# Image scores copied out by VectorE instead of ScalarE, and the second pair's norm products and rounding issued ahead of a slot's last filler work, in a two-layer image-prompted cross-attention

## The chip, the cores and the metric

The kernel runs on one core of one Trainium2 chip. The time is the device time of one execution in microseconds (us). Three runs of the kernel before gave a median of 1542.27 us, from 1538.93 to 1542.37 us.

## The reference

Two cross-attention layers follow each other on 16 images of 256 query rows and 320 channels, with 20 heads of 16 channels. The context of an image has 252 text tokens and 4 image tokens of 512 channels. The second layer, which is the one that the change touches, computes (cut to what matters):

```python
q = heads(hidden_states @ W_q)                       # also k_t, v_t, k_ip, v_ip from the context
probs_t = softmax(einsum('bhsd,bhtd->bhst', q, k_t) * attn_scale)
text_out = einsum('bhst,bhtd->bhsd', probs_t, v_t)
attn_scores = einsum('bhsd,bhnd->bhsn', q, k_ip) * attn_scale
qsem = l2norm(einsum('bhst,bte->bhse', probs_t, text_ehs))
sem = einsum('bhse,bne->bhsn', qsem, l2norm(ip_ehs))
probs_ip = softmax(attn_scores + 0.5 * sem) * spatial_mask
out = (text_out + einsum('bhsn,bhnd->bhsd', probs_ip, v_ip)) @ W_out + b_out + residual
```

The norm of `qsem` is not computed from `qsem`: with the Gram matrix G of the text tokens, its square is p G p for each row p of the (not yet normalized) probabilities.

## The kernel before, in words

The work is cut into slots. A slot k is one image and four heads: slots 0 to 79 belong to layer 0, slots 80 to 159 to layer 1, five to an image, so that 16 images follow each other with five slots each. The main loop (L1139) goes through the parts of `slot1(k)` in order. A part that is a function issues instructions; a part that is a number n calls `fill(k + n)`, which issues all filler work that is due by then: the next image's keys and tokens (`prod`, L212), query and output projections (`project`, L520), and the rest. TensorE's instructions stay in the order in which they are issued. The order on VectorE, ScalarE and GpSimd is made by a scheduler that honours data dependencies and the manual ones that `queued` adds: `anchor(x)` remembers an instruction as the last anchored one of its engine, `queued(x)` puts x behind that one.

In slot k of layer 1 the following happens.

- `both1(k, t)` for the two halves t of 128 rows: the turned scores of slot k (L788, tiles `T`, two PSUM banks) and the row scores of slot k + 2 (L793, tile `S`, two banks, of which there is one only). VectorE takes the row maxima of the text scores from `S` (L794). ScalarE takes the exponentials of the turned scores (L799). `image_scores` copies the 4 image scores of each of the four heads, 16 numbers in each partition, out of `S` into `sr` (L811, on ScalarE). The matmuls of half 1 into `S` can begin when both readers of half 0 are done.
- `attend1(k - 2)`, between the two halves: probabilities times values (L862) and, as the last term of the same sum, the squared norms (L864). Its second operand `wt` is summed by GpSimd for pair u = 0 and by VectorE for pair u = 1 (L854).
- `rounded1(k, u)`: ScalarE rounds the exponentials to a narrow type (L839, tile `ctb`, two of them), GpSimd takes the remainder (L840, tile `wt`).
- `norm1(k - 1, u, n)`: the product with one block column of the Gram matrix G (L849, four matmuls for n = 0, three for n = 1); VectorE multiplies it with `wt` (L852) and the two columns are added (L854).
- `maxima(k + 2)`: the maxima are transposed (L827), cast by ScalarE (L829) and sent by two DMAs from ScalarE's queue into the rows of `qs` (L831).

Of the filler work, these lines play a part below: `keys1`, where ScalarE casts and VectorE subtracts (L147, L148, tile `kst`); `tokens1`, which makes the values and the Gram matrix of the next image (L478 to L499, tiles `v1t` and `gm`; L499 is VectorE's last read of its last PSUM tile); and the split of the context (L147 and L148 on GpSimd, tile `cta`).

The PSUM tiles are declared with one to three buffers each, but the eight banks are handed out anew as tiles are asked for (`auto_bufs`), so that a tile's bank can be the one that any other kind of tile has left.

Of the kernel before, what the change touches and what calls it, by code (L numbers as in the profile page):

```python
# [10 lines left out]
AF = mybir.ActivationFunctionType  # L11
# [17 lines left out]
SCALE = 0.25  # L29
# [8 lines left out]
NS = B * NG  # L38
# [10 lines left out]
def xattn2(  # L49
# [27 lines left out]
    nc = tc.nc  # L77
# [11 lines left out]
    def bank(tag="X"):  # L89
        return ps.tile([128, 512], F32, tag=tag, name=tag, bufs=BANKS[tag])  # L90

    def scores():

        return ps.tile([128, 1024], F32, tag="S", name="S", bufs=1).rearrange("p (h t) -> p h t", h=4)
# [4 lines left out]
    def buf(tag, shape, dtype=F32, bufs=1, name=None):  # L99
        if tag in ("wB", "wD", "vr", "raw"):  # L100
            return sb.tile(shape, dtype, tag=tag, name=name or tag, bufs=bufs)
        size = 1
        for d in shape[1:]:
            size *= d
        if tag not in slots:
            slots[tag] = [0, dtype] + [const_tile([128, max(size, words.get(tag, 0))], f"{tag}_{i}", dtype) for i in range(bufs)]
        n, kind, *ring = slots[tag]
        assert kind == dtype and len(ring) == bufs, tag
        slots[tag][0] += 1
        t = ring[n % bufs][: shape[0], :size]  # L110
        names = "abcd"[: len(shape) - 1]
        if len(names) > 1:
            t = t.rearrange(f"p ({' '.join(names)}) -> p {' '.join(names)}", **dict(zip(names, shape[1:])))
        return t
# [17 lines left out]
    def queued(inst, *behind):  # L132

        for other in behind or [anchors.get(inst.ins.engine)]:
            if other is not None:
                tc.add_manual_dep(
                    inst.ins, other.ins.name, mybir.DependencyInfo(mybir.DependencyClass.NoSync, mybir.DependencyReason.DATA), reason="order"
                )
        return inst

    def anchor(inst):
        anchors[inst.ins.engine] = inst
        return inst
# [460 lines left out]
    QK, P, W, R = {}, {}, {}, {}  # L604
# [76 lines left out]
    def attend0(k):  # L681
        b, g = divmod(k, NG)
        v, pv = get("v0", b), bank("P")
        for vt in range(3):
            values0(k, pv, v, vt)
        settle0(b, g, pv)
# [87 lines left out]
    def both1(k, t):  # L774

        a = k + 2 < 2 * NS and QK[k + 2] 
        c = NS <= k < 2 * NS and QK[k]
        if a:
            if t == 0:
                maxes[k + 2] = buf("mn", [128, 4, 4], FR, bufs=2)[:, :2]  # L780
            sp = scores()
        if c:
            st = [bank("T").rearrange("p (h t) -> p h t", h=2) for u in range(2)]
            lo = (0, DUP)[t]
            for j in range(2):
                for u in range(2):
                    rows = slice(64 * u, 64 * u + KS1)
                    mm(st[u][:, j], c[1][rows, j, lo : lo + 128], c[0][rows, j], start=True, stop=True)  # L788
        if a:
            for j in range(2):  # L790
                for u in range(2):
                    rows = slice(64 * u, 64 * u + XROW)
                    mm(sp[:, 2 * u + j], a[0][rows, j, t * 128 : (t + 1) * 128], a[1][rows, j], start=True, stop=True)  # L793
            anchor(nc.vector.tensor_reduce(maxes[k + 2][:, t], sp[:, :, :T1], axis=AX.X, op=ALU.max))  # L794
        if c:
            for u in range(2):
                if t == 0:
                    P[k, u] = buf("P", [128, 2, 2, S], bufs=SIZES["NP"]) if (k - NS) % 3 else last_stack([128, 2, 2, S], F32, u)
                anchor(queued(nc.scalar.activation(P[k, u][:, t], st[u], AF.Exp, scale=SCALE)))  # L799
        if a:  # L800
            image_scores(k + 2 - NS, t, sp)

    sims = {}

    def image_scores(n, t, sp):
        b, g = divmod(n, NG)
        if (g, t) == (0, 0):
            sims[b] = buf("sr", [128, 2, 4, NG, NIP], bufs=2)
        sr = sims[b]
        src = sp.rearrange("p (u j) t -> p u j t", u=2)[:, :, :, T1:]  # L810
        anchor(nc.scalar.copy(sr[:, t, :, g].rearrange("p (j u) n -> p u j n", u=2), src))  # L811
        if (g, t) == (NG - 1, 1):
            later(0.3, lambda: image_scores_out(b))

    def image_scores_out(b):
        sid = dram.tile([S, 4, NG * NIP], F32, tag="sid", name="sid", bufs=2)
        dma(sid.rearrange("(t p) s c -> p t (s c)", p=128), sims[b].rearrange("p t s g n -> p t (s g n)"))
        si = results["si", b] = buf("si", [128, 8, NG * NIP], bufs=2)
        parts = sid.rearrange("(f r) s c -> r s f c", r=32)
        for s in range(4):  # L820
            later(1.3, lambda s=s: dma(si[32 * s : 32 * s + 32], parts[:, s]))
# [13 lines left out]
    def rounded1(k, u):  # L835
        R[k, u] = buf("ctb", [128, 2, 2, S], FR, bufs=SIZES["CTB"], name="ph")
        W[k, u] = buf("wB", [128, 2, 2, S], bufs=SIZES["WB"], name="wt")
        for t in range(2):
            nc.scalar.activation(R[k, u][:, t], P[k, u][:, t], AF.Copy, scale=0.5)  # L839
            anchor(nc.gpsimd.tensor_sub(W[k, u][:, t], P[k, u][:, t], f(R[k, u][:, t])))  # L840
# [3 lines left out]
    def norm1(k, u, n):  # L844

        gm = get("t1", k // NG - B)[1]
        yp = bank().rearrange("p (h t) -> p h t", h=2)
        for i, (gb, kt) in enumerate(blocks[n]):
            mm(yp, gm[:, gb], R[k, u][:, kt], start=i == 0, stop=i == len(blocks[n]) - 1)  # L849
        w = W[k, u]  # L850
        product = yp if n and u else w[:, n]
        nc.vector.tensor_mul(product, yp, w[:, n])  # L852
        if n:
            (nc.vector if u else nc.gpsimd).tensor_add(w[:, 0], w[:, 0], product)  # L854

    def attend1(k):
        b, g = divmod(k - NS, NG)
        v, pv = get("t1", b)[0], bank("P")
        for n in range(2):
            for s in range(4):  # L860
                h = V1W * (4 * g + s)
                mm(pv[32 * s : 32 * s + 32, :S], v[:, n, h : h + 32], P[k, s % 2][:, n, s // 2], start=n == 0, stop=False)  # L862
        for s in range(4):
            mm(pv[32 * s : 32 * s + 32, :S], zone, W[k, s % 2][:, 0, s // 2], start=False, stop=True)  # L864
        settle1(b, g, pv)

    def slot1(k):
        last = k - 1 if NS < k <= 2 * NS else None
        mine = k < 2 * NS
        if k == NS:  # L870
            yield lambda: maxima(k + 1)
        yield lambda: both1(k, 0)
        if k == NS:
            yield lambda: attend0(k - 1)
        if k > NS + 1:
            yield lambda: attend1(k - 2)
        yield lambda: both1(k, 1)
        if last:
            yield lambda: norm1(last, 0, 0)
        yield 0.33  # L880
        if last:
            yield lambda: norm1(last, 0, 1)
        if mine:
            yield lambda: rounded1(k, 0)
        yield lambda: stacks(k + LEAD)
        if last:
            yield lambda: norm1(last, 1, 0)
        yield 0.67
        if last:
            yield lambda: norm1(last, 1, 1)  # L890
        if mine:
            yield lambda: rounded1(k, 1)
        yield lambda: maxima(k + 2)
        yield 1.0

# [124 lines left out]
    def later(slots, make):  # L1020
        delayed.append((clock[0] + slots, make))
# [26 lines left out]
    for c in range(B // 2):  # L1048
        n, k = 10 * c, [("k0", c)] if c else []
# [11 lines left out]
    for b in range(B):  # L1061
        n = NS + 5 * b
# [17 lines left out]
    def stacks(k, parts="KQ"):  # L1080
        if 0 <= k < NS:
            stacks0(k, parts)
        elif k < 2 * NS and "K" in parts:
            stacks1(k)

    def ahead(k, t):
        if k < NS:
            score0(k, t)
        else:
            both1(k - 2, t)  # L1090

    def maxima(k):
        if k < 2 * NS:
            (maxima0 if k < NS else maxima1)(k)
# [43 lines left out]
    with tc.manual_schedule(engines=PINNED):  # L1138
        for k in range(2 * NS + 2):  # L1139
            clock[0] = k  # L1140
            for part in (slot0 if k < NS else slot1)(k):
                if callable(part):
                    part()
                else:
                    fill(k + part)
        fill(999)
# [81 lines left out]
```

## Time and profile before

| | |
|---|---|
| median of 3 runs | 1542.27 us |
| the profiled execution | 1542.67 us |
| its span, first to last instruction | 1540.9 us |
| VectorE busy | 1167.0 us (76%) |
| ScalarE busy | 966.5 us (63%) |
| GpSimd busy | 1144.5 us (74%) |

The profile names engines PE (TensorE's matmuls), PEld (its weight loads), DVE (VectorE), ACT (ScalarE), POOL (GpSimd) and SP (SyncE, whose rows here are DMA issues). A row of a timeline has the start in us from the span's start, the duration in us, engine, line, operation, the tiles written and read, the shape, how often, and in square brackets the idle time ahead of it with what ended it. Layer 1 runs from about 700 us to the end.

### The profile page before, as it was taken

Reading aid. Unit: us, or ns where it says so; the run is one execution under the profiler, and the core shown is the slowest. Engines: PE = TensorE matmul, PEld = TensorE weight load, DVE = VectorE, ACT = ScalarE, POOL = GpSimd, SP = SyncE. Lnnn points to the kernel's source line nnn. Section 1 sums busy time; section 2 is a strip of 40 time slices with the busy share of each in tenths; the row PEclk is TensorE's granted clock in tenths of the full one; section 3 lists DMA queues with packets and bytes.
Section 4 is the critical chain, followed back from the end, with each engine's and each line's share of the span. In section 5 each row is a group of like instructions: output and inputs, shape, how many; then the busy total and the mean of one; then the engine's idle time right before and its main releaser. Section 6 shows DMA issues by size and latency. Waiting matters only on the chain.

```text
span 1540.9 us, 35237 instructions
## 1 busy us (share of the span) xinstructions
PE 1461.3 (95%) x12522; PEld 1194.7 (78%) x12522; DVE 1167.0 (76%) x2424; ACT 966.5 (63%) x2233; POOL 1144.5 (74%) x1161
## 2 busy tenths in 40 slices
PE   7789999999999998899999999999999999999997
PEld 6778888888888887677777777777777777777765
DVE  5457676767776778877888788878877887888796
ACT  5557676767676766656656555655665566556562
POOL 3259797979797867886777777777777787777685
PEclk9899999999999999999999999999999999999999
DMA  7656565656565665464424443434344434433311
GB/s 218 164 170 173 161 173 165 176 164 178 156 192 144 169 195 134 122 195 145 142 80 142 117 135 107 132 114 146 104 136 120 136 111 129 127 110 107 110 34 57
DMA packets 226971, 215.38 MB, mean 140 GB/s; under 512 B 49714, under 2 KB 210708, under 8 KB 226796
## 3 DMA queue, kind: packets, MB, share of 16 engines
q1 hardware_dynamic: 225056, 211.83, 47.9%
q8 instruction: 100, 1.64, 0.5%
q10 hardware_dynamic: 1740, 1.30, 0.3%
q14 instruction: 75, 0.61, 0.1%
HBM read 122.17 MB, written 89.49 MB: 137 GB/s over the span
## 4 chain that ended last, share of the span: by engine, by line
PE 61%; DVE 12%; ACT 7%; POOL 7%; DMA 7%; issue 3%; ACTq 2%; SPq 1%; POOLq 0%; DVEq 0%
PE X L212 19%; PE X L849 10%; PE X L520 8%; PE P L711 7%; PE S L650 5%; DVE mn L794 4%; PE T L673 4%; POOL wt L840 3%; PE S L793 2%; ACT ctb L839 2%; ACTq L831 2%; POOL wt L854 1%; DMA sid<-sr 1%; POOL cta L148 1%; PE X L569 1%
## 5 line engine op out<-in xcount | busy, mean ns | idle before, releaser
L679 POOL TENSOR_TENSOR P<-P,rs 128x512 f32<-128x512 f32 x320 | 412.1, 1310 | 158.8 <-ACT P L676 158.7
L840 POOL TENSOR_TENSOR wt<-P,ctb 128x512 f32<-128x512 f32 x212 | 270.8, 1296 | 94.5 <-ACT ctb L839 93.5
L849 PE MATMUL X<-ctb,gm 128*128 128x512 f32 x1120 | 308.8, 405 | 0.4 <-DVE ho L750 0.4
L676 ACT ACTIVATE P<-T 128x512 f32<-128x512 f32 x320 | 174.8, 593 | 103.8 <-PE T L673 94.6
L849 PEld LDWEIGHTS X<-ctb,gm 128*128 128x128 f32 x1120 | 195.8, 188 | 41.3 <-DVE ho L750 0.6
L794 DVE TENSOR_REDUCE mn<-S 128x4 fp32r<-128x1008 f32 x160 | 191.0, 1194 | 18.1 <-PE S L793 17.7
L852 DVE TENSOR_TENSOR wt<-X,wt 128x512 f32<-128x512 f32 x240 | 164.4, 686 | 38.7 <-PE X L849 36.7
L839 ACT ACTIVATE ctb<-P 128x512 fp32r<-128x512 f32 x212 | 124.8, 626 | 45.5 <-PE X L849 43.2
L652 DVE TENSOR_REDUCE mn<-S 128x4 fp32r<-128x716 f32 x160 | 142.4, 890 | 0.0
L711 PE MATMUL P<-P,vr 128*32 128x256 f32 x1920 | 123.8, 388 | 4.8 <-DVE mx L575 2.6
L799 ACT ACTIVATE P<-T 128x512 f32<-128x512 f32 x212 | 114.5, 593 | 7.4 <-PE T L788 7.3
L520 PE MATMUL X<-hq,wE 128*128 128x256 f32 x768 | 112.8, 291 | 3.9 <-ACT hq L509 3.4
L520 PE MATMUL X<-ho,wF 128*128 128x256 f32 x768 | 108.6, 284 | 3.3 <-DVE ho L752 2.7
L520 PEld LDWEIGHTS X<-hq,wE 128*128 128x128 f32 x768 | 103.0, 194 | 7.1 <-ACT hq L509 3.9
L520 PEld LDWEIGHTS X<-ho,wF 128*128 128x128 f32 x768 | 101.9, 190 | 8.2 <-DVE ho L752 3.1
L212 PE MATMUL X<-cta,wA 128*128 128x252 f32 (+1 forms) x720 | 100.6, 286 | 5.7 <-ACT wA L147 5.4
L854 POOL TENSOR_TENSOR wt<-wt 128x512 f32<-128x512 f32 x80 | 103.4, 1293 | 0.6 <-DVE wt L852 0.6
L840 POOL TENSOR_TENSOR wt<-qsl,ctb 128x512 f32<-128x512 f32 x54 | 69.1, 1291 | 41.2 <-ACT ctb L839 40.9
L212 PEld LDWEIGHTS X<-cta,wA 128*128 128x128 f32 x720 | 92.0, 193 | 7.4 <-ACT wA L147 5.7
L722 DVE STREAM_TRANSPOSE nt<-P 128x512 f32<-128x512 f32 x80 | 57.0, 713 | 49.9 <-PE P L711 49.9
L651 DVE TENSOR_REDUCE mn<-S 128x4 fp32r<-128x308 f32 x160 | 74.6, 467 | 23.7 <-PE S L650 23.5
L811 ACT COPY sr<-S 128x16 f32<-128x16 f32 x160 | 27.7, 173 | 102.1 <-DVE mn L794 100.9
(217 smaller groups left out, 3373.9 us busy)
## 6 DMA issues: line engine op xcount, KB each, us to landing
qd<-q SPq DMA_DIRECT2D x96, 384.0 KB
kd<-kst SPq DMA_DIRECT2D x73, 256.0 KB
rawc<-in_cT_dram SPq DMA_DIRECT2D x60, 256.0 KB
ks<-kd SPq DMA_DIRECT2D x160, 96.0 KB
qs<-qd SPq DMA_DIRECT2D x160, 96.0 KB
qs<-qd SPq DMA_DIRECT2D x60, 192.0 KB
ks<-kd SPq DMA_DIRECT2D x60, 192.0 KB
kd<-kst SPq DMA_DIRECT2D x21, 512.0 KB
```

The lines of the kernel that those rows point to most:

```text
L212: last = mm(out, lhs(a, k), rhs(b, k), start=i == 0, stop=i == len(terms) - 1)
L520: mm(pp, w(s, k, slice(m * 128, (m + 1) * 128)), a[:, t], start=i == 0, stop=i == len(terms) - 1)
L652: anchor(nc.vector.tensor_reduce(mn[:, t, 1], sp[:, :, T0:], axis=AX.X, op=ALU.max))
L676: exp = anchor(nc.scalar.activation(pt, st[p], AF.Exp, scale=SCALE))
L679: anchor(nc.gpsimd.tensor_mul(pt, pt, rs[:, t : t + 1].to_broadcast([128, 2, S])))
L711: mm(pv[32 * s : 32 * s + 32, o : o + S], v[:, vt, h : h + 32], P[k, s // 2][:, t, s % 2], start=vt < 2, stop=vt != 1,)
L794: anchor(nc.vector.tensor_reduce(maxes[k + 2][:, t], sp[:, :, :T1], axis=AX.X, op=ALU.max))
L839: nc.scalar.activation(R[k, u][:, t], P[k, u][:, t], AF.Copy, scale=0.5)
L840: anchor(nc.gpsimd.tensor_sub(W[k, u][:, t], P[k, u][:, t], f(R[k, u][:, t])))
L849: mm(yp, gm[:, gb], R[k, u][:, kt], start=i == 0, stop=i == len(blocks[n]) - 1)
L852: nc.vector.tensor_mul(product, yp, w[:, n])
L854: (nc.vector if u else nc.gpsimd).tensor_add(w[:, 0], w[:, 0], product)
```

## The change

The image scores' copy moves from ScalarE to VectorE, issued directly after the maxima and queued behind them. The exponentials are no longer queued behind the last anchored ScalarE instruction. In `slot1`, `norm1(last, 1, 1)` and `rounded1(k, 1)` come ahead of `fill(k + 0.67)`, so that the products (0, 1), (1, 0) and (1, 1) stand next to each other on TensorE.

```diff
@@ both1 @@
             anchor(nc.vector.tensor_reduce(maxes[k + 2][:, t], sp[:, :, :T1], axis=AX.X, op=ALU.max))
+            image_scores(k + 2 - NS, t, sp)
         if c:
             for u in range(2):
                 if t == 0:
                     P[k, u] = buf("P", [128, 2, 2, S], bufs=SIZES["NP"]) if (k - NS) % 3 else last_stack([128, 2, 2, S], F32, u)
-                anchor(queued(nc.scalar.activation(P[k, u][:, t], st[u], AF.Exp, scale=SCALE)))
-        if a:
-            image_scores(k + 2 - NS, t, sp)
+                anchor(nc.scalar.activation(P[k, u][:, t], st[u], AF.Exp, scale=SCALE))
@@ image_scores @@
-        anchor(nc.scalar.copy(sr[:, t, :, g].rearrange("p (j u) n -> p u j n", u=2), src))
+        anchor(queued(nc.vector.tensor_copy(sr[:, t, :, g].rearrange("p (j u) n -> p u j n", u=2), src)))
@@ slot1 @@
         yield lambda: stacks(k + LEAD)
         if last:
             yield lambda: norm1(last, 1, 0)
-        yield 0.67
-        if last:
             yield lambda: norm1(last, 1, 1)
         if mine:
             yield lambda: rounded1(k, 1)
+        yield 0.67
         yield lambda: maxima(k + 2)
         yield 1.0
```

## The prediction, made before the changed kernel ran

> **What bounds the kernel now.** I read the page first, then the stretch of layer 1 in which the images follow each other evenly, then TensorE's waits in layer 1, and then the timeline of one image's five slots.
>
> ```profile
> span 1540.9 us, 35237 instructions
> ...
> PE 1461.3 (95%) x12522; PEld 1194.7 (78%) x12522; DVE 1167.0 (76%) x2424; ACT 966.5 (63%) x2233; POOL 1144.5 (74%) x1161
> ...
> PE 61%; DVE 12%; ACT 7%; POOL 7%; DMA 7%; issue 3%; ACTq 2%; SPq 1%; POOLq 0%; DVEq 0%
> ```
>
> ```profile
> 800.00:1400.00 600.00, 583.82 (x4770) 456.32 (x4769) 481.94 (x909) 358.24 (x876) 448.24 (x493) 1.00 0.42 124
> ```
>
> ```profile
> PE S L793 <- ACT sr L811: 16.7, 44, 1.2
> PE P L864 <- POOL wt L854: 8.5, 17, 1.4
> ```
>
> The chain of waits lies on TensorE for 61% of the span, and between 800 and 1400 us TensorE is busy 583.82 of 600 us (the columns are PE, PEld, DVE, ACT, POOL, clock, DMA). So TensorE bounds this stage, with a little over 16 us of gaps here, and only these gaps are to be had. The waits in layer 1 name two kinds: the second half's row scores (L793) wait for ScalarE's copy to give back tile `S`, 44 times, and the norms (L864) wait for GpSimd's sum. VectorE is busy 481.94 of 600 us, more than ScalarE's 358.24.
>
> Waits hide matmuls that run one behind another where four could run beside each other, so I measure the loss directly: the time from a slot's first L793 to its second, which holds the same matmuls in every slot (L793, L862, L864, L788). These are TensorE's rows of the five slots of one image:
>
> ```profile
> 975.25 0.40 PE L793 MATMUL S<-ks,qs 48*128 48x256 f32 x4
> ...
> 977.01 0.50 PE L788 MATMUL T<-qs,ks 50*128 50x256 f32 x4
> 977.36 0.47 PE L793 MATMUL S<-ks,qs 48*128 48x256 f32 x4
> ...
> 984.53 0.40 PE L793 MATMUL S<-ks,qs 48*128 48x256 f32 x4
> ...
> 987.82 0.50 PE L793 MATMUL S<-ks,qs 48*128 48x256 f32 x4 [0.26 <-ACT sr L811]
> ...
> 994.51 0.40 PE L793 MATMUL S<-ks,qs 48*128 48x256 f32 x4
> ...
> 997.22 0.50 PE L793 MATMUL S<-ks,qs 48*128 48x256 f32 x4
> ```
>
> ```profile
> 1006.18 0.40 PE L793 MATMUL S<-ks,qs 48*128 48x256 f32 x4
> ...
> 1008.97 0.50 PE L793 MATMUL S<-ks,qs 48*128 48x256 f32 x4 [0.52 <-ACT sr L811]
> ...
> 1016.58 0.40 PE L793 MATMUL S<-ks,qs 48*128 48x256 f32 x4
> ...
> 1019.16 0.50 PE L793 MATMUL S<-ks,qs 48*128 48x256 f32 x4 [0.18 <-ACT sr L811]
> ```
>
> The distances are 2.11, 3.29, 2.71, 2.79 and 2.58 us. The first slot has no wait in this stretch, so the others lose 1.18, 0.60, 0.68 and 0.47 us: 2.93 us for an image, 47 us for 16 images. That is the most that this change can gain here.
>
> **The change part by part.** First the copy.
>
> ```profile
> L794 DVE TENSOR_REDUCE mn<-S 128x4 fp32r<-128x1008 f32 x160 | 191.0, 1194 | 18.1 <-PE S L793 17.7
> ...
> L811 ACT COPY sr<-S 128x16 f32<-128x16 f32 x160 | 27.7, 173 | 102.1 <-DVE mn L794 100.9 <-DVE nt L908 1.0
> ...
> L394 DVE COPY rn<-X 128x64 f32<-128x64 f32 x1 | 0.2, 206 | 0.0
> ```
>
> 160 copies of 173 ns leave ScalarE, with 100.9 us in which its queue stood behind the maxima. ScalarE has idle time, so by itself that frees nothing. VectorE gets 160 copies that the trace does not show there. The nearest row is its copy of 64 elements out of PSUM, 206 ns; that is the upper bound, and the lower is the 75 ns by which the maxima's 1194 ns exceed the 1.12 us to the next start shown below, as overlap alone. I take 0.15 us, nearer to the upper row: 24 us more on VectorE, which takes it in the stretch above from 80% to about 84%.
>
> The Trainium skill (Perfetto Trace Analysis, "Optimizing Scalar/DVE Operations") speaks against this move: it puts the fixed cost of an operation on PSUM at about 125 ns for VectorE and 51 ns for ScalarE, and advises moving work to ScalarE where VectorE is saturated. By it 160 copies would add 160 x (125 + 17) ns = 23 us to VectorE and take only 10 us from ScalarE, an estimate; the sum with all of it on the path would be 23 us higher. The trace has 206 against 173 ns, a smaller difference than the page's.
>
> Now the slots, where both parts meet. VectorE's rows in the first and second slot:
>
> ```profile
> 975.70 1.21 DVE L794 TENSOR_REDUCE mn<-S 128x4 fp32r<-128x1008 f32 x1 [1.09 <-PE S L793]
> ...
> 985.24 0.35 DVE L495 SCALAR_TENSOR_TENSOR gm<-X,tmask,gm 128x128 fp32r<-128x128 f32 x1 [0.37 <-ACT gm L494]
> 985.51 0.34 DVE L499 SCALAR_TENSOR_TENSOR gm<-X,tmask,gm 128x124 fp32r<-128x124 f32 x1
> 985.77 0.68 DVE L854 TENSOR_TENSOR wt<-wt,X 128x512 f32<-128x512 f32 x1
> 986.36 1.20 DVE L794 TENSOR_REDUCE mn<-S 128x4 fp32r<-128x1008 f32 x1
> 987.48 0.44 DVE L908 STREAM_TRANSPOSE nt<-P 128x256 f32<-128x256 f32 x1
> ```
>
> A free VectorE begins the maxima 0.45 us after L793 (975.25 to 975.70) and is through with them 1.12 us later (986.36 to 987.48). With the copy (0.15) and a hand-over (0.05) `S` is free 1.77 us after L793, ahead of the 2.11 us at which TensorE wants it: 0.34 us of slack. In the second slot VectorE was not free: L495, L499 and L854 stand ahead, L854 because its product (1, 1) was issued last. Once (1, 1) is earlier, L854 is done before the slot. But the order of the changed kernel's instructions shows something new: L495 and L499 now stand behind the maxima and the copy of half 0, and the second of the four L788 of half 1 waits for L499, because its `T` tile has got the bank that L499 reads last. That wait ends at 0.45 + 1.12 + 0.15 + 0.27 (L495 to L499) + 0.34 (L499) + 0.05 = 2.38 us. TensorE wants the bank at 1.76 us (975.25 to 977.01). So 0.62 us of loss stays of 1.18: **gain 0.56 us**. Queued behind this wait are the rest of L788 and L793; for them wait the exponentials, which have slack.
>
> The third slot waits for GpSimd:
>
> ```profile
> 991.20 1.79 PE L849 MATMUL X<-ctb,gm 128*128 128x512 f32 x7
> ```
>
> ```profile
> 991.71 1.15 ACT L839 ACTIVATE ctb<-P 128x512 fp32r<-128x512 f32 x2
> ```
>
> ```profile
> 992.48 2.53 POOL L840 TENSOR_TENSOR wt<-P,ctb 128x512 f32<-128x512 f32 x2 [0.79 <-ACT ctb L839]
> 994.97 1.28 POOL L854 TENSOR_TENSOR wt<-wt 128x512 f32<-128x512 f32 x1
> 996.21 1.28 POOL L148 TENSOR_TENSOR cta<-rawc,cta 128x512 fp32r<-128x512 f32 x1
> ```
>
> Product (0, 1) at 991.20 lets the rounding start, then two remainders and the sum follow on GpSimd until 996.25, and L864 starts there. The change leaves this order as it is: the same matmuls lie between (0, 1) and L864, only in another order, so the 0.60 us stays. The context's subtraction (L148, 996.21) moves behind the second pair's remainders (2.53 us, as L840 above), and ends at about 1000.0 instead of 997.5. The next image's keys need it from their eighth matmul:
>
> ```profile
> 999.80 0.85 PE L212 MATMUL X<-cta,wA 128*128 128x252 f32 x6
> ```
>
> That is the second half of the twelve, whose second matmul is the eighth: about 999.9. I put this at 0 to 0.2 us lost. **Loss 0.1 us.**
>
> The fourth and the fifth slot:
>
> ```profile
> 1005.43 1.30 ACTq L831 DMA_DIRECT2D qs<-mt  x2
> ...
> 1006.78 0.37 ACT L147 CAST kst<-X 128x252 fp32r<-128x252 f32 x1 [1.38 <-PE S L793]
> ...
> 1007.18 0.42 DVE L148 TENSOR_TENSOR kst<-X,kst 128x252 fp32r<-128x252 f32 x1 [0.61 <-ACT kst L147]
> ...
> 1007.52 1.20 DVE L794 TENSOR_REDUCE mn<-S 128x4 fp32r<-128x1008 f32 x1
> ```
>
> ```profile
> 1017.03 0.69 DVE L854 TENSOR_TENSOR wt<-wt,X 128x512 f32<-128x512 f32 x1
> 1017.64 1.20 DVE L794 TENSOR_REDUCE mn<-S 128x4 fp32r<-128x1008 f32 x1
> ```
>
> In the fourth, the maxima start 1.34 us after L793, behind a subtraction that waits for a cast that waits for two DMA issues in ScalarE's queue. The changed order has the same chain. Only the copy's way is shorter: 1007.52 to 1008.97 is 1.45 us, and becomes 1.12 + 0.15 + 0.05 = 1.32. **Gain 0.1 us.** In the fifth, L854 alone delays the maxima from 0.45 to 1.06 us. With (1, 1) ahead of the projection it is done in time; the query's subtraction that now stands last ends at about the same 0.45 us. **Gain 0.47 us**, the whole loss. The first slot has none to give.
>
> Costed at nothing: the exponentials without `queued` (the order shows them at the same place, and their tiles come free in time), the second pair's earlier rounding (its remainders end earlier on GpSimd, where nothing waits for them), and the three products next to each other (each waits in the changed order for banks left long before). The cover is TensorE's filler work between the products and the next slot; without it, a product would wait for VectorE's turn of 0.69 us (as L854 above has it) on its bank.
>
> The sum for an image is 0.56 - 0.1 + 0.1 + 0.47 = 1.03 us, for 16 images 16.5 us. Against the profiled execution's 1542.67 us that is 1526.2; this execution lies 0.4 us above the median of the runs, so I say **1526 us**. With the bounds of the copy (0.075 to 0.206 us), of the third slot and of the fourth (0 to 0.2), the image gains 0.8 to 1.3 us, 13 to 21 us in all; the first and last image have other gaps, so this case has 1518 to 1534 us.
>
> **The rivals.**
>
> *VectorE falls behind (slower).* In the first and second slot VectorE has the most to do, and its reserve is the 1.09 us of idle time ahead of the maxima at 975.70, plus gaps like 0.37 us. Two slots bring four copies (0.6 to 0.8 us), and the order puts one more operation of the image softmax (L962) into the second slot. If that reserve is gone, each operation that comes late shifts the maxima of the next half and so L793, and the copies are on the path: 160 x 0.17 = 27 us against the 16.5 gained, 1553 us. It decides from the point where the maxima of the second slot start more than 0.76 us after L793. For it speaks the in-order queue; against it that the long L854 leaves the place ahead of the maxima. Chance 0.20.
>
> *GpSimd sets the pace (no change).* Every gain ahead of (0, 1) moves TensorE closer to the sum that it waits for in the third slot, and L864 in the other slots follows GpSimd's sum by little. GpSimd is busy 448 of 600 us, but its chain from (0, 1) to the sum is 5.05 us (991.20 to 996.25) whatever TensorE does. If it takes back 0.4 and more of each gain, an image gains at most 0.2 us: 1539 to 1544 us. Chance 0.15.
>
> *Everything goes (faster still).* If the scheduler's bank for L788 is free in time after all and the fourth slot's chain shortens with ScalarE's relief, up to 47 us go: about 1500 us. The order speaks against it. Chance 0.05.
>
> That the change does not do what it says is excluded by the order: products and copies stand where the diff puts them.
>
> **How the numbers follow.** The forecast has 0.60. About 0.3% (5 us) is what a measurement of this kernel can tell from no change. Faster: 0.60 + 0.05 = 0.65; same 0.15; slower 0.20. The forecast's own range of 1518 to 1534 has to reach to the others: down to 1510 for part of the larger gain, up to 1549 for no change and the milder half of the slower case.
>
> **What would show it.** After the change: the distances of the two L793 should read about 2.1, 2.7, 2.8, 2.7 and 2.1 us; among TensorE's waits the one for ScalarE's `sr` is gone, one of L788 for VectorE's `gm` L499 is new, about 0.6 us 13 times (so often the order has it), and the one for GpSimd's L854 is no smaller; VectorE's copies take about 0.15 us. I am wrong if the maxima of the second or fifth slot start late, if L788 waits for nothing, or if new waits appear at the products L849.

## The result, and the profile after

The changed kernel takes 1528.29 us (median of 4 runs, 1525.50 to 1530.94), the kernel before 1541.28 us (4 runs, 1538.93 to 1542.37): ratio 0.9917, 95% interval 0.9891 to 0.9944, some 13 us faster. The profiled execution takes 1525.5 us; it is the fastest of the four.

The page of the changed kernel, its span, its engines and the shares of the chain of waits:

```profile
span 1523.4 us, 35306 instructions
...
PE 1452.4 (95%) x12522; PEld 1196.4 (79%) x12522; DVE 1180.6 (77%) x2584; ACT 956.0 (63%) x2073; POOL 1142.2 (75%) x1161
...
PE 72%; POOL 10%; DVE 6%; DMA 5%; issue 3%; ACT 3%; SPq 0%; ACTq 0%; POOLq 0%; DVEq 0%
```

160 instructions have changed sides: VectorE has 2584 instead of 2424, ScalarE 2073 instead of 2233. On the chain that ended last TensorE has risen from 61 to 72%, ScalarE has fallen from 7 to 3% and VectorE, although it got work, from 12 to 6%. GpSimd has gone from 7 to 10%.

The window 800 to 1400 us (columns as before: PE, PEld, DVE, ACT, POOL, clock, DMA), and TensorE's waits in all of layer 1:

```profile
800.00:1400.00 600.00, 587.23 (x4851) 467.02 (x4850) 501.23 (x1042) 358.60 (x780) 455.63 (x501) 1.00 0.42 126
```

```profile
PE P L863 <- POOL wt L853: 8.7, 18, 1.0
PE S L793 <- DVE sr L810: 7.4, 15, 0.9
PE T L788 <- DVE gm L499: 3.2, 13, 0.2
```

In the same 600 us TensorE now runs 4851 matmuls instead of 4770: 1.7% more work in the same time, while its busy time rose by 0.6% only. The wait for ScalarE's copy of `S`, 16.7 us 44 times before, is now one for VectorE's copy, 7.4 us 15 times. The wait of L788 for L499 is new, 13 times, as the order had it. The wait for GpSimd's sum is where it was.

TensorE's rows for the five slots of one image, first L793 and second L793 of each:

```profile
970.20 0.40 PE L793 MATMUL S<-ks,qs 48*128 48x256 f32 x4
...
972.31 0.40 PE L793 MATMUL S<-ks,qs 48*128 48x256 f32 x4
...
979.40 0.40 PE L793 MATMUL S<-ks,qs 48*128 48x256 f32 x4
...
981.16 0.38 PE L788 MATMUL T<-qs,ks 50*128 50x256 f32 x1
981.79 0.47 PE L788 MATMUL T<-qs,ks 50*128 50x256 f32 x3 [0.24 <-DVE gm L499]
982.01 0.48 PE L793 MATMUL S<-ks,qs 48*128 48x256 f32 x4
...
988.77 0.41 PE L793 MATMUL S<-ks,qs 48*128 48x256 f32 x4
990.59 0.64 PE L863 MATMUL P<-wt,zone 128*32 128x256 f32 x8 [0.41 <-POOL wt L853]
...
991.50 0.40 PE L793 MATMUL S<-ks,qs 48*128 48x256 f32 x4
...
1000.68 0.40 PE L793 MATMUL S<-ks,qs 48*128 48x256 f32 x4
...
1003.40 0.50 PE L793 MATMUL S<-ks,qs 48*128 48x256 f32 x4 [0.46 <-DVE sr L810]
...
1011.04 0.40 PE L793 MATMUL S<-ks,qs 48*128 48x256 f32 x4
...
1013.27 0.40 PE L793 MATMUL S<-ks,qs 48*128 48x256 f32 x4
```

The distances are 2.11, 2.61, 2.73, 2.72 and 2.23 us; before they were 2.11, 3.29, 2.71, 2.79 and 2.58. So the second and the fifth slot have become shorter, the third and the fourth hardly at all. The table has the medians over the 11 images in the middle, for every kernel of this study: the distance in each slot, and the period from image to image.

| kernel | slot 1 | 2 | 3 | 4 | 5 | period |
|---|---|---|---|---|---|---|
| before | 2.10 | 3.00 | 2.71 | 2.79 | 2.64 | 52.53 |
| after | 2.11 | 2.61 | 2.72 | 2.74 | 2.22 | 51.76 |
| e1, copy alone | 2.11 | 2.90 | 3.01 | 2.63 | 2.48 | 52.50 |
| e2, products alone | 2.33 | 2.53 | 2.72 | 2.77 | 2.19 | 51.92 |
| e3, copy thrice | 2.60 | 2.88 | 3.40 | 3.48 | 2.64 | 54.27 |
| e9, two spare copies | 2.10 | 2.55 | 2.67 | 2.13 | 2.22 | 51.89 |
| e8, maxima sent by SyncE | 2.11 | 2.10 | 2.69 | 2.74 | 2.22 | 51.75 |
| e4, tokens early | 2.11 | 2.67 | 2.72 | 2.74 | 2.23 | 52.59 |
| e5, sum first | 2.11 | 2.61 | 2.58 | 2.11 | 2.11 | 51.87 |
| e7, tokens and sum | 2.11 | 2.67 | 2.58 | 2.11 | 2.11 | 52.61 |
| e10, e8 and the mask later | 2.11 | 2.10 | 2.70 | 2.10 | 2.23 | 51.10 |
| e11, e10 and the split earlier | 2.11 | 2.10 | 2.90 | 2.10 | 2.23 | 50.35 |
| e12, e11 and sum first | 2.11 | 2.10 | 2.90 | 2.10 | 2.11 | 50.24 |

### The profile page after: what moved, and what is told of

Same layout as the page of the kernel before. It is cut to its first block, busy times and chain, and to the rows that moved or that the text cites. A ratio compares the mean times of both kernels' runs of the same rounds, so it can differ in the third digit from the quotient of the medians.

```text
span 1523.4 us, 35306 instructions
## 1 busy us (share of the span) xinstructions
PE 1452.4 (95%) x12522; PEld 1196.4 (79%) x12522; DVE 1180.6 (77%) x2584; ACT 956.0 (63%) x2073; POOL 1142.2 (75%) x1161
## 4 chain that ended last, share of the span: by engine, by line
PE 72%; POOL 10%; DVE 6%; DMA 5%; issue 3%; ACT 3%; SPq 0%; ACTq 0%; POOLq 0%; DVEq 0%
PE X L212 21%; PE X L848 14%; PE X L520 10%; PE P L711 7%; POOL wt L839 6%; PE S L650 5%; PE T L673 4%; PE T L788 3%; DMA rs<-vipd 3%; PE P L861 2%; DVE mn L794 2%; PE S L793 2%; POOL wt L853 2%; PE P L863 1%; PE X L569 1%
## 5 line engine op out<-in xcount | busy, mean ns | idle before, releaser
L848 PE MATMUL X<-ctb,gm 128*128 128x512 f32 x1120 | 293.7, 402 | 0.0
L848 PEld LDWEIGHTS X<-ctb,gm 128*128 128x128 f32 x1120 | 199.5, 188 | 46.4 <-issue 0.4
L711 PE MATMUL P<-P,vr 128*32 128x256 f32 x1920 | 126.9, 395 | 5.3 <-DVE mx L575 2.8
L520 PE MATMUL X<-hq,wE 128*128 128x256 f32 x768 | 114.4, 292 | 4.7 <-ACT hq L509 3.5
L520 PE MATMUL X<-ho,wF 128*128 128x256 f32 x768 | 108.6, 284 | 4.8 <-DVE ho L752 4.0
L212 PE MATMUL X<-cta,wA 128*128 128x252 f32 (+1 forms) x720 | 105.4, 290 | 7.3 <-ACT wA L147 5.8
L520 PEld LDWEIGHTS X<-hq,wE 128*128 128x128 f32 x768 | 103.6, 194 | 9.1 <-ACT hq L509 4.0
L520 PEld LDWEIGHTS X<-ho,wF 128*128 128x128 f32 x768 | 102.0, 190 | 9.9 <-DVE ho L752 4.4
L839 POOL TENSOR_TENSOR wt<-qsl,ctb 128x512 f32<-128x512 f32 x54 | 69.2, 1293 | 51.9 <-ACT ctb L838 49.8
L853 POOL TENSOR_TENSOR wt<-wt 128x512 f32<-128x512 f32 x80 | 103.3, 1292 | 0.0
L212 PEld LDWEIGHTS X<-cta,wA 128*128 128x128 f32 x720 | 93.8, 194 | 11.9 <-ACT wA L147 6.1
L147 ACT CAST kst<-X 128x252 fp32r<-128x252 f32 (+3 forms) x94 | 35.1, 373 | 95.3 <-PE X L212 75.5
L711 PEld LDWEIGHTS P<-P,vr 128*32 128x32 f32 x1920 | 56.5, 112 | 46.6 <-issue 9.6
```

The source lines that it names most:

```text
L212: last = mm(out, lhs(a, k), rhs(b, k), start=i == 0, stop=i == len(terms) - 1)
L520: mm(pp, w(s, k, slice(m * 128, (m + 1) * 128)), a[:, t], start=i == 0, stop=i == len(terms) - 1)
L711: mm(pv[32 * s : 32 * s + 32, o : o + S], v[:, vt, h : h + 32], P[k, s // 2][:, t, s % 2], start=vt < 2, stop=vt != 1,)
```

## The experiments

All are edits of the changed kernel, except e2, which is the kernel before with the third hunk of the change. Each ratio is to runs of the kernel before that belong to the same group of runs (medians 1541.97 to 1544.22 us), so the ratios compare better than the times.

| run | us | against the kernel before (95%) |
|---|---|---|
| e1 | 1539.28 | 0.9972 (0.9959 to 0.9986) |
| e2 | 1532.41 | 0.9935 (0.9917 to 0.9953) |
| e3 | 1574.45 | 1.0206 (1.0185 to 1.0228) |
| e9 | 1526.91 | 0.9896 (0.9874 to 0.9919) |
| e8 | 1525.14 | 0.9889 (0.9870 to 0.9908) |
| e4 | 1542.72 | 0.9992 (0.9977 to 1.0007) |
| e5 | 1528.99 | 0.9897 (0.9878 to 0.9917) |
| e7 | 1539.87 | 0.9977 (0.9962 to 0.9992) |
| e10 | 1516.68 | 0.9843 (0.9814 to 0.9872) |
| e11 | 1505.31 | 0.9763 (0.9736 to 0.9790) |
| e12 | 1509.54 | 0.9773 (0.9745 to 0.9800) |

### e1 and e2: each part by itself

e1 keeps the copy on VectorE, with the exponentials no longer queued, and puts the products back:

```diff
             yield lambda: norm1(last, 1, 0)
+        yield 0.67
+        if last:
             yield lambda: norm1(last, 1, 1)
         if mine:
             yield lambda: rounded1(k, 1)
-        yield 0.67
```

> Only the first part of the change: VectorE copies the image scores, the products stay where they were. Theory (the reordered products bring the gain, because VectorE's sum of the second pair no longer stands ahead of the maxima): only the copy's shorter way is left, about 0.1 us in each of the second, fourth and fifth slot, whose distances from the first to the second L793 read about 2.9, 2.7 and 2.5 us; 16 images x 0.3 = 5 us, 1536 to 1539 us. Rival (the gain comes from ScalarE's queue, which no longer stands behind the maxima): 1528 us as with the whole change.

e2 keeps the products and puts the copy back to ScalarE (with the exponentials queued, as before):

> Only the second part: products and rounding of the second pair next to each other, the copy stays on ScalarE. Theory: the fifth slot's distance falls to 2.2 us as with the whole change, the second's to 2.5 us (L499 follows the maxima without a copy between), the fourth stays at 2.8; 1528 to 1531 us, all but some 2 us of the gain. Rival (the copy's move is needed for the gain): the fifth slot stays at 2.5 us, 1536 us or more.

Both theories come out in the total, e1 and e2 each a little above what was expected. The copy alone is worth 0.28%, some 4 us, the products alone 0.65%, some 10 us; 0.9972 x 0.9935 = 0.9907, and both together measure 0.9917. So about a quarter to a third of the total is the copy's (with the exponentials, which e1 does not separate from it) and the rest the products'. Where they gain is another matter. The products shorten the second and the fifth slot (3.00 to 2.53, 2.64 to 2.19). The copy alone shortens the second, the fourth and the fifth by 0.10 to 0.16 each, but lengthens the third by 0.30, which was not expected, and the median period falls by 0.03 only. Where e1's 4 us lie is not shown. From the first image's first L793 to the sixteenth's, the profiled executions take 778.1 us before, 777.3 in e1, 769.3 in e2 and 764.1 after; from there to the end of the span 49.8, 47.1, 49.0 and 46.3. But these are single executions, of which four of the changed kernel lie 5.4 us apart, and the last stretch takes 46.2 to 50.6 us over all kernels of this study, 49.7 in e8, which has both parts.

Beside the products the copy is worth 0.16 us of the median period (51.92 to 51.76), and the table shows where: in the first slot, which e2 lengthens from 2.10 to 2.33 and the whole change does not (in the second slot 0.08 of it goes again). ScalarE in e2, in a first slot whose first L793 is at 972.43:

```profile
974.31 0.34 ACT L946 ACTIVATE a<-a 128x160 f32<-128x160 f32 x1 [0.59 <-POOL a L944]
974.55 0.15 ACT L811 COPY sr<-S 128x16 f32<-128x16 f32 x1
```

The copy stands on ScalarE behind an exponential of the image softmax (L946), which waits for GpSimd, and starts 2.12 us after L793; the second L793 follows at 974.76. It is so in all 11 images. In the changed kernel VectorE's copy starts 1.57 us after L793. The prediction, which gave the first slot nothing to win, did not see that the products alone would have lost there what the copy wins back. In the third slot of e1 VectorE loses for another reason. Its rows, with the first L793 at 993.00:

```profile
993.68 0.65 DVE L853 TENSOR_TENSOR wt<-wt,X 128x512 f32<-128x512 f32 x1
994.25 1.20 DVE L794 TENSOR_REDUCE mn<-S 128x4 fp32r<-128x1008 f32 x1
995.37 0.41 DVE L750 TENSOR_TENSOR ho<-X,ho 128x256 fp32r<-128x256 f32 x1
995.70 0.16 DVE L810 COPY sr<-S 128x16 f32<-128x16 f32 x1
```

With the products at their old place L853 stands ahead of the maxima as before the change (they start 1.25 us after L793), and the scheduler, which need only keep the copy behind the maxima, has put an operation in between. The second half's L793 comes at 996.01, behind the copy.

### e3 and e9: what does a copy cost?

e3 makes the copy three times, into the same place:

```diff
+        for again in range(3):
-        anchor(queued(nc.vector.tensor_copy(sr[...], src)))
+            anchor(queued(nc.vector.tensor_copy(sr[...], src)))
```

> The changed kernel with each image-score copy made three times on VectorE, so 320 copies more of 0.164 us each, about 0.12 us from start to start. Theory (VectorE has slack except where TensorE waits for it): two more copies lengthen the second and the fourth slot by 0.24 us each, the first slot's 0.34 us of slack holds them, the fifth loses 0.1: 0.5 to 0.6 us for an image, 8 to 10 us in all, 1536 to 1538 us. Rival (VectorE is close to setting the pace in layer 1): all of 320 x 0.12 to 0.16 us is paid, 38 to 52 us, 1566 us or more.

It came out some 45 us above the changed kernel (2.9% by the ratios): the theory fell, and the time is the one of the rival. But VectorE's timeline in e3 shows another reason than the rival's:

```profile
985.49 1.21 DVE L794 TENSOR_REDUCE mn<-S 128x4 fp32r<-128x1008 f32 x1 [1.71 <-PE S L793]
986.61 0.16 DVE L811 COPY sr<-S 128x16 f32<-128x16 f32 x1
986.69 0.31 DVE L942 TENSOR_REDUCE m<-a 128x40 f32<-128x160 f32 x1
986.92 0.16 DVE L811 COPY sr<-S 128x16 f32<-128x16 f32 x1
987.00 0.44 DVE L907 STREAM_TRANSPOSE nt<-P 128x256 f32<-128x256 f32 x1
987.36 0.14 DVE L811 COPY sr<-S 128x16 f32<-128x16 f32 x1
```

The scheduler put other work between the copies, so that `S` is free only at 987.50, 2.01 us after the maxima began, instead of about 1.3. The run does not price three copies alone; with them it prices a tile that is held. e9 therefore makes two more copies of the same numbers into spare tiles, directly behind the first:

```diff
         anchor(queued(nc.vector.tensor_copy(sr[...], src)))
+        for again in spare:
+            anchor(queued(nc.vector.tensor_copy(again.rearrange(...), src)))
```

> The changed kernel with two more copies of the same image scores into spare tiles, which the order puts directly behind the first one in most places, so that they neither wait for it nor hold the score tile for other work. With three copies into one tile the order had put other VectorE work between them, and the tile was held for up to 2.0 us after the maxima's start. Theory (that run's 46 us came from the held tile, and a copy by itself costs about 0.08 us of VectorE's time from start to start): 320 more copies cost 0.1 to 0.2 us in the slots that wait for the tile, 5 to 10 us in all, 1533 to 1539 us. Rival (VectorE sets the pace in layer 1, and any work added is paid): 320 x 0.14 us again, 1570 us.

VectorE's group of the added copies in e9:

```profile
L813 DVE COPY spare<-S 128x16 f32<-128x16 f32 x320 | 39.3, 164 | 0.0
```

320 more copies, 39.3 us of busy time, and the kernel takes no longer than the changed one (0.9896 against 0.9917, the intervals overlap). With this edit the scheduler also ordered other work differently (slot 4 is at 2.13, and the rest of the third slot is 0.86 longer, where the keys' L212 waits ten times 0.66 us for VectorE, as in e5 below; in the second slot L788 does not wait for L499), so the total alone would prove little; but slots 1, 3 and 5 read 2.10, 2.67 and 2.22, about as without the copies. So VectorE's load is not what a copy costs in this stage. What costs, as e3 and the third slot of e1 have it, is how long the one `S` is held where TensorE waits for it.

### e8: do ScalarE's DMA issues delay the fourth slot?

The prediction's chain in the fourth slot begins with two DMA issues in ScalarE's queue. e8 issues them from SyncE:

```diff
-            nc.scalar.dma_start(
+            nc.sync.dma_start(
```

> The changed kernel with the two DMAs of the maxima of layer 1 issued by SyncE instead of ScalarE. Theory (the fourth slot's loss is the chain cast behind two DMA issues on ScalarE, then VectorE's subtraction, then the maxima): the fourth slot's distance falls from 2.7 to 2.1 or 2.2 us, the others stay; 13 images x 0.5 = 7 us, 1521 us. Rival (the maxima of the fourth slot are late for another reason, or SyncE's queue holds the loads up): the distance stays at 2.7 us, or new waits of L788 and L793 for DMAs appear; 1528 us or more.

The fourth slot stays at 2.74, so taking away the DMA issues is not enough. VectorE in the fourth slot, of the changed kernel and then of e8:

```profile
1000.57 1.16 DVE L961 TENSOR_TENSOR rs<-rs,nt 128x384 f32<-128x384 f32 x1 [0.66 <-DMA rs<-vipd]
1001.66 0.41 DVE L148 TENSOR_TENSOR kst<-X,kst 128x252 fp32r<-128x252 f32 x1
1001.99 1.19 DVE L794 TENSOR_REDUCE mn<-S 128x4 fp32r<-128x1008 f32 x1
1003.10 0.16 DVE L810 COPY sr<-S 128x16 f32<-128x16 f32 x1
```

```profile
999.16 0.84 DVE L961 TENSOR_TENSOR rs<-rs,nt 128x384 f32<-128x384 f32 x1 [1.00 <-DMA rs<-vipd]
999.92 0.41 DVE L148 TENSOR_TENSOR kst<-X,kst 128x252 fp32r<-128x252 f32 x1
1000.25 1.19 DVE L794 TENSOR_REDUCE mn<-S 128x4 fp32r<-128x1008 f32 x1
```

In both, an operation that the prediction did not look at stands ahead: the mask of the image values (L961 here, L963 before), which waits for a DMA, with the subtraction L148 and the maxima behind it in VectorE's order. ScalarE's cast for L148 starts at 998.70 in e8 and is done long before 999.92; there it is the mask that sets the time. In the changed kernel the chain of the prediction stands close behind the mask. ScalarE's rows there:

```profile
999.55 1.31 ACTq L830 DMA_DIRECT2D qs<-mt  x2
...
1000.90 0.37 ACT L147 CAST kst<-X 128x252 fp32r<-128x252 f32 x1 [1.38 <-PE T L788]
```

Before, the subtraction followed 0.40 us behind the start of its cast (1006.78 to 1007.18); here it follows 0.76 behind (1000.90 to 1001.66), because the mask still runs. So without the mask, but with the DMA issues on ScalarE, the maxima would come some 0.36 us earlier, an estimate from these rows, and still some 0.5 us later than on a free VectorE. The fourth slot is held by both, one behind the other.

In the second slot something else happened. With e8 the distance falls to 2.10, so the wait for L499 is gone, which the edit was not meant to do, but the period stays at 51.75. TensorE's waits in e8 (850 to 1400 us):

```profile
PE X L520 <- POOL hq L510: 5.4, 11, 0.8
```

The half microsecond has gone to L520, the next image's query projection, a few matmuls later: it waits for a split that GpSimd makes (L510), and the rest of the second slot grows from 6.77 to 7.30 us. In the changed kernel L520 came late enough not to wait. **Here too two waits stood one behind the other**, and only the first was visible.

### e4, e5 and e7: taking away the waits that the list names

e4 issues the last part of `tokens1`, with L495 and L499, earlier:

```diff
-        task(("t1", b), shifted(n, -3.67, -3, -2.67, -2.33), lambda b=b: tokens1(b), ...)
+        task(("t1", b), shifted(n, -3.67, -3, -2.67, -2.67), lambda b=b: tokens1(b), ...)
```

> The changed kernel with the last piece of the next image's token products (the Gram matrix's second half, whose last reader is VectorE's L499) issued at the filler call ahead of the products instead of behind them. In the order its PSUM tile is read out before the second slot starts, and no L788 waits for L499 any more. Theory (this new wait is what keeps 0.5 us of the second slot's loss): the second slot's distance falls from 2.61 to 2.1 us, 13 images x 0.5 = 6.5 us, 1521 to 1523 us. Rival (VectorE is as late anyway, or the products then wait for banks): the distance falls by less than 0.2 us or TensorE waits at L848; 1527 us or more.

The theory fell: the wait for L499 is gone and so is the gain of the whole change. L520 waits for L510 (5.5 us, 10 times; the rest of the second slot takes 7.50 us instead of 6.77), and the second slot is no shorter (2.67): L793 waits for `S` 21 times instead of 10. For in e4 VectorE's sum L853 stands ahead of the second slot's maxima again, as in the kernel before, and they start 1.26 us after L793 instead of 0.44. On TensorE all 24 token matmuls (L212) of this stretch now run ahead of the last three products, where the changed kernel has twelve ahead and twelve behind, so L853, the remainders and GpSimd's L510 come later against the second slot (L510 starts 4.54 us after its first L793 in one image, 3.77 in the changed kernel). So e4 does not take away the one wait alone; it also undoes what the change won in this slot.

e5 queues GpSimd's sum for pair 0 ahead of the pair's second remainder, so that L863 finds it (cut; `sums[k]` is that sum of slot k, kept by `norm1`):

```diff
+            sub = anchor(nc.gpsimd.tensor_sub(W[k, u][:, t], ...))
+            if t and not u and k - 1 in sums:
+                queued(sub, sums[k - 1])
```

> The changed kernel with GpSimd's sum of the first pair ordered ahead of the second remainder of that pair, where it stood behind both. Theory (the third slot's loss is GpSimd's chain rounding, two remainders, sum; nothing else is late there): the sum ends 1.25 us earlier, the third slot's distance falls from 2.7 to 2.1 or 2.2 us and TensorE's wait for the sum goes; 14 images x 0.55 = 8 us, 1520 us. Rival (GpSimd's whole load sets the pace): the wait moves to a later user of GpSimd's results, L848 or L863 in the next slot, and the time stays within 2 us of 1528.

All waits for the sum go, slots 4 and 5 come down to 2.11, and the time is the same as without. The third slot comes down to 2.58 only, where 2.1 or 2.2 was expected: behind the sum stands a second limit, VectorE's transposes L742, behind which the maxima start 1.18 us after L793, as they do in the changed kernel. The list of TensorE's waits in e5 (850 to 1400 us) has the rest:

```profile
PE X L212 <- DVE ho L752: 6.6, 10, 0.7
PE S L793 <- DVE sr L810: 3.1, 10, 0.3
```

The keys' projection L212, ahead of the fourth slot, takes a PSUM bank whose last reader is VectorE's L752. The wait has moved from inside the fourth slot to the matmuls before it (the rest of the third slot takes 10.2 us instead of 9.18). The fourth slot begins later by that, and its maxima start 0.50 us after L793 instead of 1.32: the mask and the cast have the time that they lacked. e7 has both edits and comes out as e4 does (1539.87 us), since e4's loss is in it:

> Both edits together on the changed kernel: the Gram matrix's second half ahead of the products, GpSimd's sum ahead of the second remainder. Theory (the losses of second and third slot are two independent waits on TensorE's path): the gains add up to 13 to 15 us, 1513 to 1516 us. Rival (one of them only uncovers the other, since TensorE reaches the sum earlier): no more than the larger of the two alone, about 1520 us.

### e10, e11 and e12: all that stands in one place

e10 is e8 with the mask queued behind the last anchored VectorE instruction, so that it no longer stands ahead of the maxima:

```diff
-        nc.vector.tensor_mul(vb, vb, w1["bmask"])
+        queued(nc.vector.tensor_mul(vb, vb, w1["bmask"]))
```

> The changed kernel with the maxima's DMAs on SyncE and with VectorE's masking of the image values (L961 there, which waits for a DMA for 0.8 us and takes 1.0 us) queued behind the maxima, where it stood ahead of those of the fourth slot. Theory (this masking, and not ScalarE's DMA issues, is what stands last ahead of the fourth slot's maxima): the fourth slot's distance falls from 2.74 to 2.1 or 2.2 us, 13 images x 0.55 = 7 us against the run with SyncE alone, 1518 us. Rival (VectorE has too much to do there, whatever the order): the distance stays above 2.6 us, or what is won is waited for in the next slot; 1525 us.

The theory held: the fourth slot goes to 2.10 and the period from 51.75 to 51.10; the total, 1516.68 us, is clear of the changed kernel's. This shows what held the fourth slot with SyncE issuing the DMAs: the mask. The late mask without e8's edit was not run; by the estimate above it would be held by the cast. What is left in e10 is led by the wait behind the second slot:

```profile
PE X L520 <- POOL hq L510: 5.2, 11, 0.5
PE P L863 <- POOL wt L853: 2.9, 7, 0.7
PE S L793 <- DVE sr L810: 1.7, 3, 0.6
```

e11 adds an earlier due time for the split, so that GpSimd makes L510 ahead of the remainders:

```diff
-        task(("o1", b), shifted(n, -7.67, -7, -6.67, ...), lambda b=b: open1(b), ...)
+        task(("o1", b), shifted(n, -8, -7.67, -6.67, ...), lambda b=b: open1(b), ...)
```

> The same, and the next image's query split (GpSimd's L510) is issued one filler call earlier, which puts it ahead of the four remainders on GpSimd instead of behind them. Theory (with L788's wait for L499 gone, the second slot is held only by L520's wait for L510, 0.5 us each): that wait goes, the rest of the second slot falls from 7.30 to 6.8 us, 7 us less than the run before it, 1511 us. Rival (GpSimd's total work sets the pace of the image): the wait moves to GpSimd's sum in the second or third slot, less than 2 us gained.

TensorE's waits in e11, in the same window:

```profile
PE S L793 <- DVE sr L810: 5.8, 11, 0.6
PE P L863 <- POOL wt L853: 0.2, 1, 0.2
```

1505.31 us, some 6 less than expected: 0.9763 of the kernel before, and the best version of this study. The wait for L510 is gone, the rest of the second slot falls to 6.59 us, and the period by another 0.75 us. The third slot's wait has changed its owner: instead of the sum, TensorE now waits for `S` (1.7 us in e10, 5.8 here), since the maxima there start 1.51 us after L793, behind L742 on VectorE. Its distance is 0.20 longer, its rest 0.20 shorter, so the slot as a whole costs what it did. e12 adds the sum of e5:

> The same, and GpSimd's sum of the first pair ahead of that pair's second remainder. Alone this brought nothing: the third slot's wait for the sum went, but a matmul of the next keys then waited for VectorE's L752 in the bank it had got, 0.7 us. Theory (that was the bank given there, not a limit of an engine): with another order the third slot's distance falls to 2.2 us and its rest stays at 9.2 us, 6 us less than the run before it, 1505 us. Rival (TensorE runs into the close of the image on ScalarE and VectorE there whatever the bank): the rest of the third slot grows by what the distance loses, and the time stays.

The theory fell: the third slot stays at 2.90, because it no longer waits for the sum but for `S`, and nothing more comes of it (1509.54 us, the intervals overlap), though the fifth slot falls to 2.11.

## Why the prediction was right, point by point

The forecast of 1526 us held, and so did the cause behind most of it, the second and the fifth slot: 1528.29 us was measured, 13.0 us below the kernel before where 16 were foretold.

**The distances and the sum.** Foretold were 2.1, 2.7, 2.8, 2.7 and 2.1, the medians are 2.11, 2.61, 2.72, 2.74 and 2.22. As terms of the sum the medians give 0.39 us in the second slot (foretold 0.56), a loss of 0.24 in the third with its rest (0.1), 0.05 in the fourth (0.1) and 0.42 in the fifth (0.47): 0.62 us instead of 1.03. With small changes in the rests of the other slots the median period fell by 0.77 us, 12 us for 16 images. The image shown in the prediction had lost more in its second slot than the median one (3.29 against 3.00), so part of the difference is the choice of the image. The two profiled executions differ by more, 17.5 us: 14.0 from the first to the sixteenth image, since the first, the last and some others gain more than the median one, and 3.5 behind that, which no term of the sum has. So the total agrees better than its terms do, and that much is luck.

**Second slot: right in its mechanism, its end met by luck.** The wait of L788 for L499 was to come 13 times and does, and it was to end 2.38 us after L793; it ends at 981.79, 2.39 after 979.40. VectorE's rows there:

```profile
979.84 1.21 DVE L794 TENSOR_REDUCE mn<-S 128x4 fp32r<-128x1008 f32 x1 [0.48 <-PE S L793]
980.97 0.17 DVE L810 COPY sr<-S 128x16 f32<-128x16 f32 x1
981.05 0.34 DVE L495 SCALAR_TENSOR_TENSOR gm<-X,tmask,gm 128x128 fp32r<-128x128 f32 x1
981.30 0.34 DVE L499 SCALAR_TENSOR_TENSOR gm<-X,tmask,gm 128x124 fp32r<-128x124 f32 x1
```

L495 starts 0.08 us behind the copy where 0.15 was taken, and the hand-over from the end of L499 (981.64) to L788 takes 0.15 where 0.05 was taken; the two errors cancel. The list of waits gives 3.2 us in all, a quarter of a microsecond each time, but the distance of 2.61 against 2.11 says 0.50. In the first slot the four L788 start two by two (1.76, 1.77, 1.99 and 1.99 us after L793); here one starts at 1.76, two at 2.39 and the last at 2.58. The first runs alone, a third turn is needed, and TensorE counts as busy during it. The prediction's choice to measure distances rather than to add up waits was needed here.

**The copy: the duration right, the cost taken too seriously.** VectorE's copies after the change:

```profile
L810 DVE COPY sr<-S 128x16 f32<-128x16 f32 x160 | 26.2, 164 | 0.0
```

0.164 us, foretold 0.15; VectorE is busy 501.23 of 600 us, 84% as foretold. That the load is harmless was argued then; e9 supports it. The Trainium skill's advice that the prediction weighed (Perfetto Trace Analysis, "Optimizing Scalar/DVE Operations"), that moving work to ScalarE may make sense where VectorE is saturated, would have pointed the wrong way for this copy: it takes 164 ns on VectorE and took 173 ns on ScalarE, and the move the other way alone (e1) gained 4 us. The same section of the Trainium skill gives its 125 and 51 ns as times for which the engine is busy, and profiled durations as about twice as long. The prediction set these figures beside profiled durations; what compares with the 125 ns is the 0.08 us from the copy's start to the next start, and this is shorter.

**Third slot: the distance right, the loss mis-sized.** GpSimd's sum stands where it stood: between 850 and 1400 us both kernels wait for it 10 times, 3.9 us. The rest of the slot grew from 8.95 to 9.18 us, a loss of 0.23 where 0.1, at most 0.2, was foretold; in all of layer 1 TensorE's weight loads wait for `cta` (L148) 4.5 us, 15 times, 0.3 us each. In e2 they do so too (4.8 us), in e1 once only (0.6 us), which fits the second pair's remainders, as foretold. But e1's rest is longer as well (9.08), for which no cause was found.

**Fourth slot: right in number, by luck; incomplete in mechanism.** The prediction took the chain of before (DMA issues, cast, subtraction, maxima) as unchanged. It is still there, but the mask has become the last thing ahead of the maxima. That the slot comes earlier now while the mask's DMA does not is the likely reason; it was not tested. The group of the mask in 850 to 1400 us, before and after:

```profile
L963 DVE TENSOR_TENSOR rs<-rs,nt 128x384 f32<-128x384 f32 x10 | 8.0, 800 | 2.3 <-DMA rs<-vipd 2.1
```

```profile
L961 DVE TENSOR_TENSOR rs<-rs,nt 128x384 f32<-128x384 f32 x10 | 10.1, 1008 | 8.1 <-DMA rs<-vipd 8.1
```

VectorE's wait for this DMA rises from 2.1 to 8.1 us. It was in the trace of before, but small. The maxima start 1.31 us after L793 instead of 1.34, which looks like an unchanged chain and is not one. The step's other part, the copy's shorter way, was foretold as 1.32 us from the maxima to L793; it is 1.41 (1001.99 to 1003.40), since the hand-over behind VectorE's copy takes 0.14 us (1003.26 to 1003.40) where 0.05 was taken.

**Fifth slot: right but for 0.1 us.** The maxima start 0.45 us after L793 (1011.04 to 1011.49), as foretold. The 0.1 us that stays is GpSimd's sum, as e5 and e12 show, in which the slot reads 2.11; it had been hidden behind the maxima.

**Costed at nothing.** The products (L848) wait for nothing in the list. The exponentials without `queued` were not run by themselves: e1 has them with the copy, e2 has neither, so what they do alone is not shown.

**The rivals.** VectorE does not fall behind in the slots that this rival named: the maxima of the second slot start 0.44 us after L793, far from the 0.76 at which it would decide. GpSimd does not set the pace through its sum, the place where the rival put it, and the time did fall. But one step further on another of its operations holds TensorE: the split L510 takes back what a shorter second slot brings (e8, e4), until it is moved (e11).

## What to carry to other kernels

Measure a stall as the distance between two points that hold the same work in every iteration, because matmuls that lose their neighbours count as busy and the list of waits understates them. When a wait is taken away, ask who is next on each in-order queue, and whether the edit has moved anything else: in e4, e5 and e8 a wait was removed for good and the time did not fall, since another took its place. With the waits for L499 and the mask both gone, e10 runs 0.7% below the changed kernel, and with the split's as well, e11 runs 1.5% below it. A short operation put behind the last reader of a scarce tile costs by the time for which it holds the tile, so see to it that nothing can be scheduled in between.

## What the runs showed of the hardware that was not expected

A VectorE copy of 16 numbers lasts 164 ns in the profile, but the next operation starts 0.08 us behind its start (980.97 to 981.05 in the second slot's rows above; 137 of the 160 copies of the changed kernel have this distance; the expectation of e3 took 0.12).

The hand-over from VectorE to a TensorE that waits, from the end of the profiled operation to the start of the matmul, took 0.15 us behind L499 and 0.14 us behind the copy; behind ScalarE's copy it took 0.06 (974.70 to 974.76 in e2).

The mask's product, whose operands all lie in SBUF, takes from 0.56 to 1.20 us in the images of the changed kernel. GpSimd beside the 1.16 us of the row at 1000.57 in the changed kernel:

```profile
1000.04 1.28 POOL L839 TENSOR_TENSOR wt<-P,ctb 128x512 f32<-128x512 f32 x1
1001.26 0.52 POOL L467 CAST kst<-kip 128x8 fp32r<-128x8 f32 x1
```

The product starts in the middle of GpSimd's remainder and ends at 1001.73, 0.47 us after the next GpSimd instruction began; that one, a cast of 8 columns, which takes 0.19 us in the median, lasts until the product ends. It looks as if each waits for the other's whole instruction. The Trainium skill (SBUF — State Buffer, "SBUF: two separate sides") says that a VectorE operation with two SBUF inputs and a GpSimd operation that reads SBUF exclude each other for a whole instruction. These rows agree; no run here was made to test it.
